# A graph kernel whose opening is put into another order: loads, node search, edge gathers and window masks

## The chip, the cores and the metric

The kernel runs on one core of a Trainium2 chip. A core has five engines that run their own instruction streams in order: TensorE (PE, matrix products and transposes, its weight loads shown apart as PEld), VectorE (DVE), ScalarE (ACT), GpSimd (POOL) and SyncE (SP). SP, ACT and POOL also issue DMA transfers, which 16 DMA engines carry out. Engines wait for each other by semaphores. The metric is device microseconds of one execution; lower is better.

## The reference, cut to what matters

There are 6250 nodes with 256 features, 100000 edges with 96 features, and `dst`, the node of each edge, in ascending order. A graph layer takes, for each node, the sum, the maximum and the mean of its edges' features, joins them to the normalised node features, and runs two dense layers. A mixture of 16 experts (two per node) follows.

```python
out1 = segment_sum(edge_attr, col)            # col = dst, sorted
cnt  = segment_sum(ones, col)
out2 = where(cnt > 0, segment_max(edge_attr, col), 0)
out3 = out1 / maximum(cnt, 1)
h = concatenate([x, out1, out2, out3, u[batch]], axis=1)     # x: layernorm of the nodes
x1 = x0 + relu(h @ W1 + b1) @ W2 + b2 + x
# then layernorm, top-2 of 16 experts, each 256 -> 512 -> 256, residual, layernorm
```

## The kernel before, in words

The 50 blocks of 125 nodes are cut into 13 groups: group 0 has two blocks, every other has four. Groups run from the last nodes to the first. For each group the hidden layer is computed in eight chunks (`hidden`, L772 and L789), then the output (`output`, L800), then the residual (L805), normalisation, gating and the scatter of rows to the experts. A list of tasks with slots (12 slots for a group) is sorted and run in order, so each engine's stream is fixed when the program is built. From slot 9 of the first two groups on, tasks are interleaved with the edge stream (`steps`, L316 to L320 on DVE), which makes running sums and maxima over all other edges and writes them to DRAM.

The nodes of groups 0 and 1 have few edges, at most 20 for a node. They don't use the edge stream. For each of their six blocks the kernel finds where a node's edges end and fetches the 20 rows before that point as a "window": 125 nodes by 20 rows by 96 features, 960 KB. This is done in steps:

- `load_all_ids` loads `dst` to 100 partitions (on ACT's queue). `block_starts` takes every 250th id and spreads it to all partitions by a matmul (L452 to L457).
- `find_block` (L486, ACT) counts for each node how many such ids lie below it; `take_blocks` (L490 to L492, DVE) makes an index, and an indirect DMA on POOL fetches the 250 ids at that place (L495, tile `gb`).
- `find_edge` (L502, ACT) counts within these ids; `bounds` (L512, L513), a pair of matmuls (`bounds_2`, L520, L521) and `index_windows` (L550 to L559, DVE) make window addresses and masks `mk`.
- `take_window` (L564, POOL) fetches a window by indirect DMA.
- `cut_window` (L572, ACT, ten small activations for half a window) or `cut_window_2` (L575, DVE, one operation for half a window) writes the window with foreign rows set to zero to a second tile. `sum_window` (L595, PE) sums it, and `add_window` (L602, DVE) folds the rest. `max_window` (L606 and L586, DVE) masks the window in place and takes its maximum; so it may begin only when the cuts have read the window. `mask_window` (L612, DVE) and `mean_window` (L617, L618, ACT) end the block.

For group 0 both engines cut, each into its own tile, `cut_w` or `cut_x`. For group 1 ACT cuts both halves, all four blocks into the one tile `cut_x`.

`check_order` (L265 to L267), `limits` and `check_fit` (L273 to L282) test whether the ids fit what the kernel was built for. The result, `misfit`, is loaded by every engine, and each branches on it (L1396, L1397): over a long block of general code that the ids of this reference don't need. Instructions on either side of that branch keep their side, save where a part of a step ended up ahead of it. Before the change, everything of groups 0 and 1 from `find_edge` on is written after the branch, although for group 0 the instructions up to L556 lie ahead of it in the streams. After the branch come also `root_x`, `scale_x` and `norm_x` (the layernorm of the nodes, L696, L702 to L704, L710), `find_block` for the four blocks of group 2 (L486), and the transposes of the normalised nodes (`turn`, L763, with the copy L764 on ACT).

DMA issues of SP and ACT share eight semaphores in turn, those of POOL eight others; a new issue waits until the transfer that used its semaphore before has landed.

Of the kernel before, what the change touches and what calls it, by code (L numbers as in the profile page):

```python
# [9 lines left out]
F32 = mybir.dt.float32  # L10
# [9 lines left out]
P = 125  # L20
# [3 lines left out]
WE = 20  # L24
# [6 lines left out]
GS = 4  # L31
# [14 lines left out]
def kernel(  # L46
# [18 lines left out]
    nc = tc.nc  # L65
# [402 lines left out]
    def more_constants():  # L468
        nc.vector.tensor_scalar(nhalf, node_i, -0.5, None, op0=OP.add)
        nc.vector.memset(rp[:, NT:], float(E))  # L470
        nc.vector.tensor_scalar(sh, row_i[:P, :P], 1.0, part_i[:P], op0=OP.add, op1=OP.is_equal)
        nc.vector.tensor_scalar(wrap, row_i[:P, :P], float(P - 1), None, op0=OP.is_equal)
        nc.vector.tensor_scalar(wrap, wrap, ident[:P, 0:1], None, op0=OP.mult)
        nc.vector.tensor_scalar(before, row_i, part_i, None, op0=OP.is_gt)
        nc.vector.memset(cnt_f, 0.0)
        nc.vector.memset(M[:, 0, :], 0.0)
# [8 lines left out]
        junk = ix.tile([P, NBK], BF16, name="junk")  # L485
        nc.scalar.activation(junk, b1r, AF.Sign, scale=-1.0, bias=nhalf[:, t:t + 1], accum_out=acc1[:, t:t + 1])  # L486

    def take_blocks(a, z):
        cols = slice(a, z)
        nc.vector.tensor_scalar(blk_f[:, cols], acc1[:, cols], float(NBK), 0.5, op0=OP.add, op1=OP.mult)  # L490
        nc.vector.tensor_scalar(blk_f[:, cols], blk_f[:, cols], -1.0, 0.0, op0=OP.add, op1=OP.max)
        nc.vector.tensor_copy(blk_i[:, cols], blk_f[:, cols])  # L492
        for t in reversed(range(a, z)):
            gbs_[t] = ix.tile([P, KB], I32, name="gb", bufs=6)
            nc.gpsimd.indirect_dma_start(out=gbs_[t], out_offset=None, in_=dst_b,  # L495
                                         in_offset=IndirectOffsetOnAxis(ap=blk_i[:, t:t + 1], axis=0))
# [75 lines left out]
            nc.scalar.activation(to[:, k, :], G[g]["win"][i][:, k, :], AF.Copy, scale=G[g]["mk"][:, i, 0, k:k + 1])  # L572

    def cut_window_2(g, i, k0, k1, to):
        nc.vector.tensor_tensor(to[:, k0:k1, :], G[g]["win"][i][:, k0:k1, :],  # L575
                                G[g]["mk"][:, i, 0, k0:k1, None].to_broadcast([P, k1 - k0, EF]), op=OP.mult)

# [99 lines left out]
    def take_x(g):  # L677
        a, z = GRP[g]
        xt = xall[:, g % XB]
        nc.sync.dma_start(xt[:, :z - a, 0:D], x[a * P:z * P].rearrange("(i p) d -> p i d", p=P))  # L680
        G[g]["xt"] = xt
# [531 lines left out]
    def at_slot(T, fn, *a, cost=0.0):  # L1213
        tasks.append((T, len(tasks), fn, a, cost))
# [21 lines left out]
    for g, (a, z) in enumerate(GRP):  # L1236
        B, n = SLOTS * g, z - a
        if g:
            if g > 1:
                at_slot(max(0, B - 17), take_x, g)  # L1240
                after = 5 if g == GW else 0
                at_slot(B - 14 + after, stats_x, g, 0, cost=1.2)
                at_slot(B - 13 + after, stats_x, g, 1, cost=1.2)
            if g > 1:
                at_slot(B - 11 + after, root_x, g)
                at_slot(B - 10 + after, scale_x, g, cost=0.5)
            at_slot(B - 9 + (4 if g == GW else 0), norm_x, g)
            for i in range(n):
                if g >= GW:
                    late = 3 if g == GW else 0  # L1250
                    at_slot(B - 10 + late + i // 2, take_edges, region[g], g, i)
                    at_slot(B - 9 + late + i // 2, take_carry, region[g], g, i)
                else:
                    for h in range(2):
                        at_slot(2 * i + h, cut_window, g, i, h * WE // 2, (h + 1) * WE // 2, None)
                        at_slot(2 * i + 1 + h, sum_half, g, i, h)
                    at_slot(2 * i + 1, max_window, g, i, cost=4.7)
                    at_slot(2 * i + 2, add_window, g, i, cost=0.9)
                    at_slot(2 * i + 2, mask_window, g, i, cost=0.4)
# [12 lines left out]
        early = GS - n  # L1272
        at_slot(B + SLOTS + 1 - early, root_b, g)
        at_slot(B + SLOTS + 2 - early, scale_b, g, cost=0.3)
        late = 0 if g >= NG - 2 else 1
        for k in range(DC):
            at_slot(B + SLOTS + 1 + k, turn_b, g, k)
        at_slot(B + SLOTS + 3 + late, logits, g)
        at_slot(B + SLOTS + 4 + late, choose, g, cost=2.4)
        at_slot(B + SLOTS + 5 + late, rank, g, cost=1.3)  # L1280
        at_slot(B + SLOTS + 6 + 2 * late, rank_2, g)
        at_slot(B + SLOTS + 7 + 2 * late, place, g, cost=1.5)
        for i in range(n):
            at_slot(B + SLOTS + 8 + 2 * late + i // 2, send, g, i)
# [37 lines left out]

    def fill_rows():

        nc.vector.memset(fill[:, D + 1:D + 5], 4.0 * NE * N)
        for h in range(SB // 128):
            nc.gpsimd.dma_start(xg_d.rearrange("(e n) d -> n e d", n=N)[h * 128:(h + 1) * 128],
                                fill[:, None, :].to_broadcast([128, NE, DR]))
# [5 lines left out]
    at_slot(SLOTS * (GW - 1) - 3, open_rows)  # L1334

    def loads_1():
        take_x(0)
        nc.sync.dma_start(w1x, w1[0:KC * 128].rearrange("(k p) h -> p k h", p=128))
        for q in range(4):
            nc.sync.dma_start(w1r[q * KR:(q + 1) * KR],  # L1340
                              w1[KC * 128:KC * 128 + KR].rearrange("k (j m n) -> k m j n", m=4, n=128)[:, q])
        take_x(1)
        load_ids(0)

    def loads_2():
# [22 lines left out]
    def windows_of(t, n):  # L1368
# [3 lines left out]
    a1, z1 = GRP[1]  # L1372
    base.append(chp.tile([P, RR, 2 * EF], F32, name="ct").rearrange("p r f -> p (r f)")[:, 0:(NT - W0) * 2 * EF]
                .rearrange("p (t f) -> p t f", f=2 * EF))
    w1u = wk.tile([P, GS, D], F32, name="xn", bufs=1).rearrange("p i d -> p (i d)")[:GF, 0:HID]
    cut_x = windows_of(xall[:, XB - 2:].rearrange("p b i d -> p (b i d)"), 1)[0]
    cut_w = w2s[:P].rearrange("p k d -> p (k d)")[:, 0:WE * EF].rearrange("p (k f) -> p k f", f=EF)
    with tc.manual_schedule():
        load_all_ids()
        loads_1()  # L1380
        nc.gpsimd.memset(base[0], 0.0)
        loads_2()
        more_constants()
        limits()
        nc.scalar.copy(gap, eps_t[0:1])
        nc.vector.memset(fill, 0.0)
        block_starts()
        check_order()
        for t in reversed(range(a, z)):
            find_block(t)  # L1390
        take_blocks(a, z)
        for t in reversed(range(a1, z1)):
            find_block(t)
        check_fit()
        take_blocks(a1, z1)
        bad_v = nc.values_load(misfit[0:1, 0:1])  # L1396
    with tc.If(bad_v != 0):  # L1397

# [39 lines left out]
        for t in range(NT - W0):  # L1438
            nc.vector.tensor_scalar(base[0][:, t, :], base[0][:, t, :], nw[:, t:t + 1], None, op0=OP.mult)
    with tc.manual_schedule():  # L1440
        global_part()
        stats_x(0, 0)
        for t in reversed(range(a, z)):
            find_edge(t)
        bounds(0)
        bounds_2(0)
        index_windows(0)
        for i in range(z - a):
            take_window(0, i, windows_of(w0p.tile([P, WE * EF], F32, name="w0"), 1)[0])
        root_x(0)  # L1450
        counts(0)
        for t in reversed(range(a1, z1)):
            find_edge(t)
        scale_x(0)
        norm_x(0)
        bounds(1)
        bounds_2(1)
        index_windows(1)
        for h in range(2):
            for w in windows_of(w1p.tile([P, 2 * WE * EF], F32, name="w1"), 2):  # L1460
                take_window(1, len(G[1].get("win", [])), w)
        stats_x(1, 0)
        stats_x(1, 1)
        root_x(1)
        scale_x(1)
        loads_3()
        for t in reversed(range(*node_cols(GW))):
            find_block(t)
# [98 lines left out]
```

## Time and profile before

| | |
|---|---|
| median of three runs | 1291.13 us (1291.03 to 1294.33) |
| the profiled execution | 1299.43 us, of which the span shown in the profile is 1297.6 us |
| busy, PE / DVE / ACT / POOL | 1113.4 / 963.4 / 612.6 / 558.8 us |
| instructions | 16883 |

Times in the profile are microseconds from the start of the span. A timeline line gives the start, the duration, the engine and line of kernel.py, the operation, what it writes and reads, the number of instructions merged, and in brackets how long the engine sat idle before it and what ended that. "DVEq" or "issue" as what ended it means the engine's own instruction queue, not another engine. In the table of stretches the columns are the length, then the busy time (and instructions) of PE, PEld, DVE, ACT and POOL, then PE's granted clock, the mean busy share of the 16 DMA engines, and GB/s.

### The profile page before, as it was taken

How to read it: one execution, taken by the hardware profiler on the slowest of the kernel's cores; microseconds unless marked ns; L12 is line 12 of the kernel's file. 1: busy time of each engine (PE TensorE's matmuls, PEld its weight loads, DVE VectorE, ACT ScalarE, POOL GpSimd, SP SyncE). 2: the span in 40 equal slices, each digit the busy share in tenths (PEclk: the TensorE clock that was granted, in tenths of full speed). 3: DMA queues.
4: the chain of work that ended last, by engine and by line, in shares of the span. 5: the costliest groups of instructions: out<-in, count | busy, mean ns of one | idle time of the engine just before them, and what ended most of it. 6: DMA issues, size and time to landing. Idle time of an engine off the chain costs nothing.

```text
span 1297.6 us, 16883 instructions
## 1 busy us (share of the span) xinstructions
PE 1113.4 (86%) x4637; PEld 783.4 (60%) x4637; DVE 963.4 (74%) x2754; ACT 612.6 (47%) x1449; POOL 558.8 (43%) x721
## 2 busy tenths in 40 slices
PE   2484796998789989899989999998999998989992
PEld 1252363655455554646646566886888777778881
DVE  4569787988988979999989422444377777778885
ACT  3484253662437542343424422432466666656662
POOL 4121142663347645375263333030145554545664
PEclk9897898999889998999999999998999999999996
DMA  5948785797779998898997331231677777778972
GB/s 163 209 108 234 206 242 160 204 242 208 216 222 267 252 244 228 235 255 228 274 260 237 90 95 42 66 100 50 195 229 228 231 238 252 254 228 254 280 259 73
DMA packets 179475, 261.25 MB, mean 201 GB/s; under 512 B 35915, under 2 KB 145963, under 8 KB 173729
## 3 DMA queue, kind: packets, MB, share of 16 engines
q1 hardware_dynamic: 140241, 202.23, 54.4%
q0 software_dynamic: 39008, 57.35, 16.1%
q8 instruction: 40, 0.66, 0.2%
q14 instruction: 74, 0.61, 0.2%
q10 hardware_dynamic: 112, 0.41, 0.1%
HBM read 146.70 MB, written 122.01 MB: 207 GB/s over the span
## 4 chain that ended last, share of the span: by engine, by line
PE 35%; DVE 13%; ACT 3%; DMA 3%; issue 3%; POOL 1%; POOLq 0%; SPq 0%; ACTq 0%; DVEq 0%
PE acc L1190 14%; PE acc L1166 11%; PE acc L772 5%; PE acc L800 3%; DVE yb L1089 2%; ACT yb L1091 2%; DVE rw L320 1%; DVE rw L317 1%; DVE rw L319 1%; DVE rw L316 1%; DMA xt<-in_x_dram 1%; ACT hb L1172 1%; DMA cg<-carry_d,next_i 1%; DMA xg_d<-xt,pos_i 1%; POOL xg_d L899 1%
## 5 line engine op out<-in xcount | busy, mean ns | idle before, releaser
L772 PE MATMUL acc<-inT,w1x 128*128 128x500 f32 (+1 forms) x832 | 369.0, 592 | 8.9 <-DVE xt L805 8.9
L772 PEld LDWEIGHTS acc<-inT,w1x 128*128 128x128 f32 x832 | 159.0, 199 | 169.7 <-issue 151.9
L1166 PE MATMUL acc<-xT,wt 128*128 128x256 f32 x912 | 223.2, 388 | 29.3 <-ACT hb L1172 25.7
L899 POOL DMA_INDIRECT xg_d<-xt,pos_i x100 | 134.4, 1344 | 250.2 <-DVE xt L895 119.8
L1190 PE MATMUL acc<-wt,hb 128*128 128x256 f32 x912 | 207.1, 380 | 0.0
L1166 PEld LDWEIGHTS acc<-xT,wt 128*128 128x128 f32 x912 | 169.2, 191 | 62.3 <-ACT hb L1172 38.1
L1190 PEld LDWEIGHTS acc<-wt,hb 128*128 128x128 f32 x912 | 174.1, 191 | 23.9
L800 PE MATMUL acc<-w2s,hT 128*125 128x256 f32 x800 | 186.5, 388 | 0.0
L800 PEld LDWEIGHTS acc<-w2s,hT 128*125 128x125 f32 x800 | 150.5, 193 | 23.7 <-issue 1.9
L1102 POOL DMA_INDIRECT g<-y_d,from_i x86 | 91.8, 1067 | 120.8 <-DMA y_d<-yb 90.5
L1135 POOL DMA_INDIRECT out_dram<-g,to_i x86 | 89.1, 1036 | 102.7 <-ACT hb L1172 86.5
L1091 ACT ACTIVATE yb<-yb,w_b 128x256 f32<-128x256 f32 x114 | 51.7, 501 | 154.0 <-DVE yb L1089 147.8
L495 POOL DMA_INDIRECT gb<-in_dst_dram,blk_i x50 | 74.1, 1483 | 114.2 <-issue 59.4
L1172 ACT ACTIVATE hb<-acc,wt 128x256 f32<-128x256 f32 x200 | 87.7, 464 | 49.5 <-PE acc L1166 41.0
L1089 DVE TENSOR_TENSOR yb<-acc,xe 128x512 f32<-128x512 f32 x57 | 39.4, 691 | 88.3 <-PE acc L1190 57.4
L794 ACT ACTIVATE hT<-acc,c 128x500 f32<-128x500 f32 (+1 forms) x104 | 60.1, 660 | 71.4 <-PE acc L789 71.4
L319 DVE TENSOR_TENSOR rw<-rw,raw 125x768 f32<-125x768 f32 x88 | 83.8, 953 | 0.0
L320 DVE TENSOR_TENSOR rw<-rw,raw 125x768 f32<-125x768 f32 x88 | 83.7, 951 | 0.0
L316 DVE TENSOR_TENSOR rw<-rw,keep 125x768 f32<-125x768 f32 x81 | 76.8, 948 | 5.0 <-DMA rows_d<-rw 4.9
L317 DVE TENSOR_TENSOR rw<-rw,bar 125x768 f32<-125x768 f32 x81 | 77.0, 950 | 0.0
L730 POOL DMA_INDIRECT at<-rows_d,first_i x44 | 61.6, 1399 | 34.2 <-issue 21.5
L737 POOL DMA_INDIRECT cg<-carry_d,next_i x44 | 63.2, 1437 | 25.7 <-issue 11.3
(313 smaller groups left out, 1577.9 us busy)
## 6 DMA issues: line engine op xcount, KB each, us to landing
wt<-in_wpack_dram SPq DMA_DIRECT2D x44, 1026.0 KB
rows_d<-rw SPq DMA_DIRECT2D x46, 960.0 KB
rows_d<-rw SPq DMA_DIRECT2D x46, 540.0 KB
raw<-in_edge_dram SPq DMA_DIRECT2D x46, 480.0 KB
xb<-xg_d SPq DMA_DIRECT2D x57, 263.0 KB
y_d<-yb SPq DMA_DIRECT2D x57, 256.0 KB
raw<-in_edge_dram SPq DMA_DIRECT2D x46, 270.0 KB
xt<-in_x_dram SPq DMA_DIRECT2D x12, 500.0 KB
```

The costliest lines, as they stand in the source:

```text
L316: nc.vector.tensor_tensor(su, prev[0], keep[c][:, :, s + j, None].to_broadcast(bcast), op=OP.mult)
L317: nc.vector.tensor_tensor(mx, prev[1], bar[c][:, :, s + j, None].to_broadcast(bcast), op=OP.min)
L319: nc.vector.tensor_tensor(su, su, x_j, op=OP.add)
L320: nc.vector.tensor_tensor(mx, mx, x_j, op=OP.max)
L772: nc.tensor.matmul(G[g]["pH"][m % 4][:, :n * P], w1x[:, k, m * 128:(m + 1) * 128], inT[:, k, :n * P], start=(k == 0), stop=False)
L800: nc.tensor.matmul(pO, G[g]["hT"][m][:, i * P:(i + 1) * P], w2s[:, m, :], start=(m == 0), stop=(m == HC - 1))
L899: d = nc.gpsimd.indirect_dma_start(out=xg_d[:, :], out_offset=IndirectOffsetOnAxis(ap=G[g]["pos"][:, i, k:k + 1], axis=0), in_=G[g]["xt"][ ...
L1102: d = nc.gpsimd.indirect_dma_start(out=g[:, h, :].bitcast(I32), out_offset=None, in_=y_d[:, :], in_offset=IndirectOffsetOnAxis(ap=BL[b]["f ...
L1135: d = nc.gpsimd.indirect_dma_start(out=out[:, :], out_offset=IndirectOffsetOnAxis(ap=BL[b]["to"][:, h:h + 1], axis=0), in_=g[:, h, :], in_ ...
L1166: nc.tensor.matmul(pB[i][:, half, :], wt[:, k * FF + m * 128:k * FF + (m + 1) * 128], xT[:, k, :], start=(k == 0), stop=(k == DC - 1))
L1172: nc.scalar.activation(hb[:, m, :], pB[i][:, half, :], AF.Relu, bias=bias)
L1190: nc.tensor.matmul(pY[:, h, :], hb[:, m, h * 128:(h + 1) * 128], wt[:, W2O + m * D:W2O + (m + 1) * D], start=(m == order[0]), stop=(m == o ...
```

## The change

- Loads: `take_x(0)` is issued on SP ahead of the ids (which are on ACT's queue); on SP, the nodes of group 1 and the small rest of W1 (`w1r`) now come before the 2 MB of W1 (`w1x`).
- `block_starts` is moved ahead of `limits`; the clearing of `fill` is moved from the opening to `fill_rows`, a task of slot 4.
- `check_order` comes after all six `find_block`, and `check_fit` after group 0's windows are requested. `take_blocks` gets an option `apart` that is not used.
- `find_edge`, `bounds`, `bounds_2`, `index_windows`, `take_window` of both groups and the node statistics `stats_x` of both are moved ahead of the branch.
- After the branch: both `root_x`, then `counts`, `scale_x`, `norm_x`, and then `global_part` (the eight products L1358 and the sum L1359).
- In group 1, ACT cuts the first half of each window and DVE the second, both in the same slot.
- `w1u` lies in a free node tile and no longer in the tile of `norm_x`.

```diff
@@ loads_1
-        take_x(0)
-        nc.sync.dma_start(w1x, ...)
+        take_x(1)
         for q in range(4):
             nc.sync.dma_start(w1r[q * KR:(q + 1) * KR], ...)
-        take_x(1)
+        nc.sync.dma_start(w1x, ...)
         load_ids(0)
@@ tasks of group 1
-                    for h in range(2):
-                        at_slot(2 * i + h, cut_window, g, i, h * WE // 2, (h + 1) * WE // 2, None)
+                    for h, fn in enumerate((cut_window, cut_window_2)):
+                        at_slot(2 * i, fn, g, i, h * WE // 2, (h + 1) * WE // 2, None)
@@ fill_rows
+        nc.vector.memset(fill, 0.0)
@@ the opening
     with tc.manual_schedule():
+        take_x(0)
         load_all_ids()
         loads_1()
...
+        nc.scalar.copy(gap, eps_t[0:1])
+        block_starts()
         limits()
-        nc.scalar.copy(gap, eps_t[0:1])
-        nc.vector.memset(fill, 0.0)
-        block_starts()
-        check_order()
         for t in reversed(range(a, z)):
             find_block(t)
         take_blocks(a, z)
         for t in reversed(range(a1, z1)):
             find_block(t)
+        check_order()
+        take_blocks(a1, z1)
+        stats_x(0, 0)
+        for t in reversed(range(a, z)):
+            find_edge(t)
+        bounds(0)
+        bounds_2(0)
+        index_windows(0)
+        for i in range(z - a):
+            take_window(0, i, ...)
         check_fit()
-        take_blocks(a1, z1)
+        stats_x(1, 0)
+        for t in reversed(range(a1, z1)):
+            find_edge(t)
+        stats_x(1, 1)
+        bounds(1)
+        bounds_2(1)
+        index_windows(1)
+        for h in range(2):
+            for w in windows_of(...):
+                take_window(1, len(G[1].get("win", [])), w)
         bad_v = nc.values_load(misfit[0:1, 0:1])
     with tc.If(bad_v != 0):
...
     with tc.manual_schedule():
-        global_part()
-        (stats, find_edge, bounds, windows of group 0)
         root_x(0)
+        root_x(1)
         counts(0)
-        (find_edge of group 1)
         scale_x(0)
         norm_x(0)
-        (bounds, windows, stats, root of group 1)
         scale_x(1)
+        global_part()
         loads_3()
```

In the resulting streams, DVE has the whole of L512 to L559 for both groups, `check_fit` and the six `stats_x` pairs ahead of its branch. PE has L1358 between the product of `check_fit` and the `bounds_2` of group 1. POOL has its six `gb` gathers and then its six windows without a branch in between, as before in that order. After the branch ACT has `norm_x(0)`, four L486, the copies L764 and the cuts, in that order as before.

More of the change, by code (lines that the diff above doesn't have):

```diff
@@ L486, in find_block, with take_blocks @@
         nc.scalar.activation(junk, b1r, AF.Sign, scale=-1.0, bias=nhalf[:, t:t + 1], accum_out=acc1[:, t:t + 1])
-    def take_blocks(a, z):
+    def take_blocks(a, z, apart=False):
         cols = slice(a, z)
@@ L492, in take_blocks, with gather_blocks @@
         nc.vector.tensor_copy(blk_i[:, cols], blk_f[:, cols])
+        if not apart:
+            gather_blocks(a, z)
+    def gather_blocks(a, z):
         for t in reversed(range(a, z)):
@@ L574, in cut_window_2 @@
     def cut_window_2(g, i, k0, k1, to):
+        to = cuts[0] if to is None else to
         nc.vector.tensor_tensor(to[:, k0:k1, :], G[g]["win"][i][:, k0:k1, :],
@@ L1336, in loads_1 @@
     def loads_1():
-        take_x(0)
-        nc.sync.dma_start(w1x, w1[0:KC * 128].rearrange("(k p) h -> p k h", p=128))
+        take_x(1)
         for q in range(4):
@@ L1341, in loads_1 @@
                               w1[KC * 128:KC * 128 + KR].rearrange("k (j m n) -> k m j n", m=4, n=128)[:, q])
-        take_x(1)
+        nc.sync.dma_start(w1x, w1[0:KC * 128].rearrange("(k p) h -> p k h", p=128))
         load_ids(0)
@@ L1374 @@
                 .rearrange("p (t f) -> p t f", f=2 * EF))
-    w1u = wk.tile([P, GS, D], F32, name="xn", bufs=1).rearrange("p i d -> p (i d)")[:GF, 0:HID]
+    w1u = xall[:, 2].rearrange("p i d -> p (i d)")[:GF, 0:HID]
     cut_x = windows_of(xall[:, XB - 2:].rearrange("p b i d -> p (b i d)"), 1)[0]
@@ L1393 @@
             find_block(t)
-        check_fit()
-        take_blocks(a1, z1)
+        check_order()
[7 more added lines that the diff above has]
+        for i in range(z - a):
+            take_window(0, i, windows_of(w0p.tile([P, WE * EF], F32, name="w0"), 1)[0])
+        check_fit()
+        stats_x(1, 0)
[6 more added lines that the diff above has]
+        for h in range(2):
+            for w in windows_of(w1p.tile([P, 2 * WE * EF], F32, name="w1"), 2):
+                take_window(1, len(G[1].get("win", [])), w)
         bad_v = nc.values_load(misfit[0:1, 0:1])
@@ L1440 @@
     with tc.manual_schedule():
-        global_part()
[L1442 to L1449, printed above, removed]
         root_x(0)
+        root_x(1)
         counts(0)
-        for t in reversed(range(a1, z1)):
-            find_edge(t)
         scale_x(0)
         norm_x(0)
[L1456 to L1464, printed above, removed]
         scale_x(1)
+        global_part()
         loads_3()
```

## The prediction

> **What bounds the kernel now.** I read the page's busy shares first: PE 86%, DVE 74%, so neither is full over the whole span. The change touches only the first 110 us, so I read the timeline there, then the stretches after it. The opening, in the timeline of the kernel before:
>
> ```profile
> 7.44 0.17 DVE L452 CAST dsf<-w 100x4 f32<-100x4 int32 x1 [1.12 <-DMA w<-in_dst_dram]
> ...
> 12.99 1.27 POOL L495 DMA_INDIRECT gb<-in_dst_dram,blk_i  x1 [7.83 <-DVE blk_i L492]
> ...
> 19.50 0.17 DVE L1359 TENSOR_TENSOR c<-ps,b1c 128x8 f32<-128x8 f32 x1 [3.29 <-PE ps L1358]
> ...
> 20.44 1.21 POOL L495 DMA_INDIRECT gb<-in_dst_dram,blk_i  x1 [4.62 <-DVE blk_i L492]
> ...
> 26.51 1.21 POOL L564 DMA_INDIRECT w<-in_edge_dram,win_i  x1 [0.31 <-issue]
> ...
> 28.15 0.18 DVE L558 TENSOR_SCALAR mk<-mk 125x40 f32<-125x40 f32 x1 [4.16 <-DVEq L1397]
> ...
> 30.55 0.17 DVE L529 TENSOR_SCALAR ne_n<-cnt 125x2 f32<-125x2 f32 x1 [1.68 <-issue]
> ...
> 31.46 1.09 ACT L710 ACTIVATE xn<-xt,nba,rsa 125x256 f32<-125x256 f32 x2 [1.88 <-issue]
> ...
> 36.37 0.30 ACT L696 ACTIVATE rsa<-mva,eps_t 125x4 f32<-125x4 f32 x1 [3.82 <-DVE mva L691]
> ...
> 41.19 2.76 ACT L572 ACTIVATE w2s<-w,mk 125x96 f32<-125x96 f32 x10 [0.26 <-DMA w<-in_edge_dram,win_i]
> ...
> 45.84 1.16 DVE L575 TENSOR_TENSOR xt<-w,mk 125x960 f32<-125x960 f32 x1 [3.50 <-DMA w<-in_edge_dram,win_i]
> 46.92 2.15 DVE L606 TENSOR_TENSOR w<-w,mk 125x1920 f32<-125x1920 f32 x1
> ```
>
> The reader is to see two paths that meet. One is the windows: requested at 26.51, first cut at 41.19, and DVE held until 45.84 by the second. The other is ACT, which at 41.19 had waited 0.26 us only: it had just come through `norm_x`, four searches and the transposes. Where the windows come earlier, ACT is late next. Group 1, by the same timeline:
>
> ```profile
> 68.50 2.16 DVE L606 TENSOR_TENSOR w<-w,mk 125x1920 f32<-125x1920 f32 x1 [8.53 <-ACT xt L572]
> ...
> 79.71 2.16 DVE L606 TENSOR_TENSOR w<-w,mk 125x1920 f32<-125x1920 f32 x1 [4.56 <-ACT xt L572]
> ...
> 98.55 2.16 DVE L606 TENSOR_TENSOR w<-w,mk 125x1920 f32<-125x1920 f32 x1 [4.75 <-ACT xt L572]
> ...
> 106.67 0.17 DVE L246 TENSOR_TENSOR keep<-di 125x48 f32<-125x48 int32 x1
> ```
>
> DVE sits idle for 17.8 us because ACT cuts both halves (2.76 us each). At 106.67 the edge stream begins. Stretches of the time that follows:
>
> ```profile
> 106.00:150.00 44.00, 21.99 (x56) 9.87 (x54) 41.42 (x87) 15.08 (x40) 9.89 (x8) 0.72 0.75 200
> 150.00:200.00 50.00, 46.65 (x175) 28.83 (x176) 40.12 (x165) 20.42 (x49) 18.41 (x18) 0.94 0.81 217
> ```
>
> DVE is busy 41.42 of 44 us, and PE waits for it; so an earlier 106.67 moves what follows.
>
> **Ids.** Let T be the moment DVE reads the ids, 7.44 before. The change takes the 2 MB of w1x from beside them and puts x of group 1 there, 500 KB. T lies between 5.4 (ids free of the 2 MB; DVE itself is free at 3.8) and 7.6 (nothing won, little lost). I take 6.9, near the measured row, since the ids had x of group 0 beside them in both.
>
> The Trainium skill ("DMA: Bandwidth & Descriptors", section on why a DMA increments its semaphore by 16) says that a transfer is spread over the largest number of engines up to 16 that divides its partitions, on SP and ACT the lowest-numbered: x with 125 partitions has five, which the ids on 99 share. By it T would stay 7.44 and the sum be 0.5 us smaller.
>
> **Windows of group 0.** The first gather leaves POOL at T+5.55, as before (12.99-7.44). Then DVE does `check_order`, three of 1.20 us, to T+8.8 (ACT's six searches at 0.755 us each end at T+7.7, so they hide beside it), and the second `take_blocks`, 0.6 us. The third gather leaves at T+9.75 instead of T+13.0, as `check_fit` and the wait for L1358 (3.29 us) are out of the way. Gathers go every 1.51 us, so the sixth is out at T+15.5 and the first window leaves at 22.7 instead of 26.51. From request to first cut took 14.7 us, to the second 17.8: landings at about 37.4 and 41 to 42, some 4 us earlier. `limits`, 2.3 us of DVE, hides beside the search; the 0.28 us of the fill is gone here and returns below.
>
> **The branch.** It now stands behind more. Gather two lands about 3.9 us after its issue (2.6 to 4.9 in the rows before), at 19.2; ACT and `bounds` give addresses 2.8 us later, 22.0, in time for POOL; masks end at 23.1. Then come `check_fit`, 3.56 us (12.58 to 16.14), and four statistics, 2.2 us: 28.9; `bounds`, 0.4. PE is in `global_part`, 3.57 us from 26.4 to 30.0, so `bounds_2` ends and DVE reads it at 31.0, 0.6 us lost to that order. Addresses and masks take 1.4 us: DVE is at its branch at 32.3 instead of 24.0, 8.3 us later. Group 1's first window leaves at 31.7 instead of 33.69, but is first needed at 60.
>
> After the branch DVE waited 4.16 us and after two further steps 1.68 us with nothing to wait for. I carry both over. Both bounds: nothing, as POOL issued across its branch after 0.31 us; and 9.37 us each, what a small gather took at 526.56 in the chain of waits, with the DMA engines busier than here. I take the rows themselves. From DVE's resume the old stream took 3.2 us to the factors of `norm_x`, less 0.5 us for the three instructions now ahead of the branch; so ACT starts `norm_x` at 39.4 instead of 31.46. From there it has 1.09 for `norm_x`, 2.9 for four searches, 1.5 for copy, transposes and copy: cut at 44.9 instead of 41.19. Before, it had 3.8 us of slack there (36.37); that cover is gone. The cut takes 2.76, so DVE's first maximum starts at 47.65 instead of 46.92: **0.7 us lost**, and the windows' 4 us not used. Two blocks of 6.0 us follow as before; group 0 ends at 59.7 instead of 58.98.
>
> The skill ("Runtime: NRT & Kernel Launch", section on instruction fetch) says that a taken branch out of the prefetched pages must fetch its target by DMA before it goes on. That speaks against this change, since six windows then load those engines; it has no figure for such a fetch.
>
> **Group 1.** Count from the end of group 0 (58.98 before, when L246 came 47.7 later). ACT's first cut ends at 6.85, as before 65.8, after copies and `keep_x`. DVE's own half, 1.16 us, lies in the idle time before. So the first maximum starts at 6.95 rather than 9.5. A block of DVE is 4.94 maximum, 0.65, 0.42, and now 1.16 for the next block's half: 7.1 us. Block one ends at 13.35 (its sum on PE is there at 12.2), the cut of block two at 14.45, b2 0.68 at 15.1. ACT has its half of block two at 11.7, so no wait. Maximum to 20.05; PE, with eight hidden products between sums and a wait for ACT's hT, has the sum at 20.3: 21.35. Cut, search index 0.6 and both clears 0.34: 23.4. ACT's half of block three came at 20.95. Maximum and fold to 29.4, cut to 30.55, the gate's work 1.95: 32.5 (ACT's half at 26.5). Maximum to 37.45. Now PE is late: its second-layer products (3.6 us) stand before the last sum, which comes at 38.8: fold to 39.9, b2 1.22, and 1.0 to L246 (as 105.7 to 106.67): 42.1 instead of 47.7. **5.6 us won.** Of the 11 us that ACT sheds and 17.8 us that DVE idled, 4.9 us are paid back as DVE's own cuts and clear, and the last sum takes part.
>
> **Sum.** -5.6 + 0.7 = -4.9 us. On the profiled execution, 1299.43 (span 1297.6 and 1.83 around it), that is 1294.5; on the median, 8.3 lower, 1286.2. The rest (w1x landing later, needed at 61; SP's branch, next needed at 48) costs nothing: at 61 the hidden products are 30 us behind any landing I can bound by the old 15.7 plus 6 for x.
>
> **Rivals.** *Slower: the branch stalls grow.* Every us that DVE resumes later comes out one for one, as ACT has no slack left. With 4.9 in hand, beyond 4.9 it is a loss, beyond 8.8 a measurable one. Both stalls at 9.37 instead of 4.16 and 1.68 are 12.9 us: 1299.1. For it: two to three windows are in flight then, where before the DMA share was about 0.35. Against: only a few fetches, and other queues got through while windows ran. *No change: the gain is given back.* One stall of 9.37 (5.2 more), or the time after 150, where DVE has 40.12 of 50 us and PE 46.65, so that a shift could end in another wait. It gives 1289 to 1292. Against it: the streams there are the same and all wait for each other, so they shift together. *More: no stall.* T at 5.4 and no fetch waits take 7.3 us from DVE's resume: ACT cuts at 37.6 to 40.4, the second window lands at 39.0 (requested at 21.2 + 17.8), and the first maximum starts at 40.4, 6.5 us earlier than before: 1279.0 at the far end, half of it 1282.6.
>
> **How the numbers follow.** Forecast 0.47 (its own range 1284 to 1289), no change 0.23, slower 0.17, more 0.13. About 0.3% (3.9 us) is what a measurement of this kernel can tell from none: 1287.3 and 1295.0. Of the forecast 0.42 lies below 1287.3, with the last case 0.55 faster; 0.05 and 0.23 make 0.28 the same; slower 0.17, of which I put two thirds above 1295. The range 1281.5 to 1295 leaves about 0.05 below and 0.13 above.
>
> **What would show it.** The third gather near 16.7 and the first window near 22.7; DVE's wait at its branch between 32 and 37; ACT's first cut near 45 with no wait for a window; DVE's waits for L572 in group 1 gone but one of about 5 us; L246 at 101 to 102. Wrong if ACT's cut waits for the windows still, if DVE resumes later than 41, or if L246 comes early and the end does not.

## The result, and the profile after

The changed kernel takes 1295.61 us (median of 20 runs, 1291.16 to 1301.12); the kernel before, run beside it, 1289.56 us (20 runs, 1285.34 to 1294.42). The ratio is 1.0046, 95% interval 1.0033 to 1.0059: about 6 us slower. The forecast was 1286.2 us, 4.9 us faster. In a later comparison, with other runs, the ratio was 1.0040 (1.0018 to 1.0062).

The timeline of the changed kernel, with the lines that answer those shown of the kernel before (start, duration, engine, line; in brackets the idle time ahead and what ended it):

```profile
6.78 0.17 DVE L452 CAST dsf<-w 100x4 f32<-100x4 int32 x1 [2.99 <-DMA w<-in_dst_dram]
...
16.89 1.21 POOL L499 DMA_INDIRECT gb<-in_dst_dram,blk_i  x1 [0.30 <-DVE bsa L695]
...
22.61 0.50 ACT L506 ACTIVATE junk<-gb,nhalf 125x250 bf16<-125x250 int32 x1 [0.45 <-DMA gb<-in_dst_dram,blk_i]
...
25.56 1.20 POOL L568 DMA_INDIRECT w<-in_edge_dram,win_i  x1 [2.92 <-DVE mk L560]
...
44.50 0.22 DVE L532 SCALAR_TENSOR_TENSOR cnt<-cnt,nf,cnt_f 125x2 f32<-125x2 f32 x1 [9.35 <-DVEq L1420]
...
51.62 0.23 DVE L537 TENSOR_SCALAR nw<-ne_n,nf 125x2 f32<-125x2 f32 x1 [6.42 <-issue]
52.14 1.09 ACT L715 ACTIVATE xn<-xt,nba,rsa 125x256 f32<-125x256 f32 x2 [20.20 <-DVE nba L708]
...
57.39 2.76 ACT L576 ACTIVATE w2s<-w,mk 125x96 f32<-125x96 f32 x10
60.19 2.16 DVE L611 TENSOR_TENSOR w<-w,mk 125x1920 f32<-125x1920 f32 x1 [5.45 <-ACT w2s L576]
...
79.12 2.16 DVE L611 TENSOR_TENSOR w<-w,mk 125x1920 f32<-125x1920 f32 x1 [4.78 <-ACT xt L576]
...
103.40 2.44 POOL L1333 DMA_DIRECT2D xg_d<-fill  x2
112.31 0.17 DVE L246 TENSOR_TENSOR keep<-di 125x48 f32<-125x48 int32 x1
119.96 11.13 SPq L329 DMA_DIRECT2D rows_d<-rw  x2
152.52 0.96 DVE L316 TENSOR_TENSOR rw<-rw,keep 125x768 f32<-125x768 f32 x1 [5.50 <-DMA rows_d<-rw]
```

Three things are to be seen. The two waits behind DVE's branch are 9.35 and 6.42 us instead of 4.16 and 1.68. ACT, which needs DVE's factor `nba`, is idle for 20.20 us, and the first maximum starts 13.3 us later than before (60.19 against 46.92). Group 1 then makes good 7.6 us: only one wait for ACT's cut is left, and from the end of group 0 to L246 it takes 40.1 us (72.25 to 112.31) where it took 47.7. Last, the edge stream, which begins 5.6 us late (112.31 against 106.67), loses about 5 us more at one place: DVE waits 5.50 us for a row buffer at 152.52, where the first profile of before had 0.55.

What was in flight when the engines stood at the branch, first in the kernel before, then in the changed one. The last three columns are PE's granted clock, the DMA share and GB/s:

```profile
20.00:25.00 5.00, 1.00 (x4) 0.91 (x4) 1.88 (x12) 3.08 (x7) 3.65 (x4) 1.00 0.40 114
25.00:30.00 5.00, 0.00 (x0) 0.00 (x0) 0.65 (x4) 2.18 (x8) 3.62 (x3) 1.00 0.35 87
```

```profile
35.00:40.00 5.00, 0.00 (x0) 0.00 (x0) 0.15 (x1) 0.00 (x0) 4.08 (x4) 1.00 0.88 199
40.00:45.00 5.00, 0.00 (x0) 0.00 (x0) 0.46 (x3) 0.00 (x0) 0.36 (x1) 1.00 0.99 220
45.00:50.00 5.00, 0.00 (x0) 0.00 (x0) 0.17 (x1) 0.00 (x0) 0.00 (x0) 1.00 1.02 257
```

In these 15 us PE and ACT do nothing and DVE 0.78 us, while the DMA engines are full.

The profiled execution of the changed kernel took 1297.04 us, less than the first profile of before (1299.43), which lay 8 to 10 us above its kernel's medians. A second profile of the unchanged kernel (below) explains this, and is the reference of the table that follows: how far the same matmul, counted from the first, starts later (+) or earlier (-) than in that second profile. It is worked out from the starts of the matmuls in the traces; "masks alone" is that kernel's second profile.

```
matmul  2nd profile  1st profile  changed  masks   masks and   changed,
        of before    of before             alone   fill early  fill early
  150      93.92       -2.70       +5.31   -8.01     -7.93       +4.77
  300     165.76       -2.92       +7.53   -7.07     -9.76       +2.82
  600     252.50       -4.83       +7.98   -7.88     -8.96       +3.73
 3300     974.16       -5.15       +8.27  -10.31    -10.83       -2.51
 4200    1167.11      +10.65       +8.28  -10.30    -10.87       -2.51
 last    1261.45      +10.77       +8.28  -10.30    -10.88       -2.50
```

The two profiles of the unchanged kernel differ by 1.2 to 7.4 us between 250 and 970 us, so the ends are read from the timed runs and the table only for where a shift arises. The four kernels that are compared below with 1302.19 us ran on a chip where the kernel before itself spread from 1283 to 1311 us, and their ratios leave out its longest runs, so that they are soft and don't follow from the medians; the traces carry the reading there.

### The profile page after: what moved, and what is told of

Read it like the earlier page. It is cut to its first block, busy times and chain, and to the rows that moved or that the text cites. A ratio compares the mean times of both kernels' runs of the same rounds, so it can differ in the third digit from the quotient of the medians.

```text
span 1295.2 us, 16845 instructions
## 1 busy us (share of the span) xinstructions
PE 1112.5 (86%) x4637; PEld 784.2 (61%) x4637; DVE 968.9 (75%) x2758; ACT 601.8 (46%) x1409; POOL 562.0 (43%) x721
## 4 chain that ended last, share of the span: by engine, by line
PE 32%; DVE 10%; ACT 4%; DMA 4%; issue 3%; POOL 1%; SPq 1%; POOLq 0%; DVEq 0%; ACTq 0%
PE acc L1195 14%; PE acc L1171 10%; PE acc L777 4%; DVE yb L1094 2%; PE acc L805 2%; DMA rows_d<-rw 2%; ACT yb L1096 2%; DVE rw L317 1%; ACT hb L1177 1%; DVE rw L320 1%; DVE rw L316 1%; DVE rw L319 1%; DMA cg<-carry_d,next_i 1%; DMA xg_d<-xt,pos_i 1%; ACT rsc L1125 1%
## 5 line engine op out<-in xcount | busy, mean ns | idle before, releaser
L805 PE MATMUL acc<-w2s,hT 128*125 128x256 f32 x800 | 190.2, 393 | 0.0
L805 PEld LDWEIGHTS acc<-w2s,hT 128*125 128x125 f32 x800 | 153.1, 196 | 24.8 <-issue 1.9
```

What stands on the lines that cost most here:

```text
L805: nc.tensor.matmul(pO, G[g]["hT"][m][:, i * P:(i + 1) * P], w2s[:, m, :], start=(m == 0), stop=(m == HC - 1))
```

## The experiments

### The masks alone, and the order alone

The kernel before with only the masks split, and the changed kernel without the split:

```diff
-                    for h in range(2):
-                        at_slot(2 * i + h, cut_window, g, i, h * WE // 2, (h + 1) * WE // 2, None)
+                    for h, fn in enumerate((cut_window, cut_window_2)):
+                        at_slot(2 * i, fn, g, i, h * WE // 2, (h + 1) * WE // 2, None)
```

> The kernel before, with only the masks of the first groups split between both engines (loads, gathers, checks and branch as before). Both theories agree here, since it measures the one term on which they rest: the second group's stage took 42.1 us in the sum and 40.5 us in the changed kernel's trace (L246 at 112.31, end of the first group at 71.83), against 47.7 us before. Theory A (the changed kernel loses its time at the branch, and the mask split is a gain): 5.6 to 7.6 us faster than before, ratio 0.994 to 0.996; the edge stream begins at about 99 to 101 us instead of 106.67. Theory B (what follows the opening gives any such gain back, so that an earlier stream start is worth nothing at the end): within 2 us of before.

> The changed kernel with the masks cut as before, by ScalarE alone: loads, order of the gathers and checks, and the late branch stay. Theory A (branch stalls): the first group's first maximum stays near 60 us (before 46.92), the group 1 stage goes back to about 47.7 us, the stream begins at about 120 us, 13 us later than before, and the end follows: 10 to 14 us slower than before, 1300 to 1304. Theory B (the stream swallows shifts of the opening): 4 to 8 us slower, as the changed kernel.

Masks alone: 1298.06 us against 1302.19, ratio 1.0026 (0.9977 to 1.0074), which settles nothing. L246 came at 98.92, as expected. (The 40.5 us of the expectation are the 40.1 us above, counted from the start of the last instruction of group 0 at 71.83.) Order alone: 1313.14 us, ratio 1.0098 (1.0062 to 1.0134). Its timeline:

```profile
43.45 0.22 DVE L532 SCALAR_TENSOR_TENSOR cnt<-cnt,nf,cnt_f 125x2 f32<-125x2 f32 x1 [8.25 <-DVEq L1420]
51.43 0.23 DVE L537 TENSOR_SCALAR nw<-ne_n,nf 125x2 f32<-125x2 f32 x1 [7.29 <-issue]
...
60.00 2.16 DVE L611 TENSOR_TENSOR w<-w,mk 125x1920 f32<-125x1920 f32 x1 [5.45 <-ACT w2s L576]
...
119.68 0.18 DVE L246 TENSOR_TENSOR keep<-di 125x48 f32<-125x48 int32 x1
```

The waits behind the branch are there without the split, and the stream starts 13.0 us later than before. So the change is two changes: an order that loses 13 us before the first maximum, and a split that wins 7.6 us behind it.

### Without the branch

The changed kernel, and the kernel before, without the `tc.If` block:

```diff
-        bad_v = nc.values_load(misfit[0:1, 0:1])
-    with tc.If(bad_v != 0):
-        ...
```

> The changed kernel without its branch and without the general code behind it, which serves other node ids than these; leaves that part out. Theory A (what the changed kernel loses, it loses in the stalls of DVE, ACT and SP at and behind the branch: 9.35 and 6.42 us on DVE): DVE's first maximum comes at 44 to 46 us instead of 60.19, bound then by the windows and ACT's cut, the stream begins near 97 to 99 us, and the kernel is 7 to 10 us faster than before. Rival C (the stalls only show a wait that is there anyway, as the landing of the windows or ACT's chain behind norm_x): the first maximum stays beyond 55 us and the time within 3 us of the changed kernel's. Rival D (the collisions in the edge stream, where DVE waits 9.7 us for rows_d instead of 4.9, come from the new load order and not from the shift): they stay, and the gain is 5 us smaller than A has it.

> The kernel before without its branch and the general code behind it; leaves that part out. It prices the branch where it stood before: VectorE's stalls were 4.16 and 1.68 us, but the windows held its first maximum until 46.92 all the same. Theory A (the cover is the landing of the windows): the first maximum comes at 43 to 46 us, 1 to 4 us earlier, and the time is 0 to 4 us below before. Rival T (the branch costs its stalls in full even there): 6 us or more below before.

The changed kernel without it: 1292.32 us against 1302.19, ratio 0.9918 (0.9878 to 0.9958). L246 came at 98.77, and DVE met no wait for its own instruction queue behind `bounds`; it waited for the windows:

```profile
40.78 1.16 DVE L580 TENSOR_TENSOR w2s<-w,mk 125x960 f32<-125x960 f32 x1 [5.99 <-DMA w<-in_edge_dram,win_i]
...
44.18 1.16 DVE L580 TENSOR_TENSOR xt<-w,mk 125x960 f32<-125x960 f32 x1 [2.09 <-DMA w<-in_edge_dram,win_i]
...
45.60 2.15 DVE L611 TENSOR_TENSOR w<-w,mk 125x1920 f32<-125x1920 f32 x1
```

This speaks against rival C: the first maximum comes 14.6 us sooner without the branch (45.60 against 60.19). Not all of it need be waits, since without the branch instructions from behind it also move forward in DVE's stream (L537 at 31.23, ahead of the addresses of group 1); the lighter windows below separate the two. The run also shows what the new order had to give without any stall: 45.60 against 46.92, 1.3 us. Rival D was half right: DVE's wait for a row buffer stayed (5.05 us at 138.53), so it isn't the branch's work, though it isn't the loads' either, as the masks alone show it too.

The kernel before without its branch: 1287.59 us against 1288.95, ratio 0.9997 (0.9974 to 1.0019). Its first maximum came at 47.45. Where the branch stood, its 5.8 us of waits cost nothing that these runs can tell (the interval ends some 3 us below before), since the windows landed later anyway. Theory A had the first maximum 1 to 4 us earlier; that was wrong, it came no earlier at all.

What the DMA engines carried from 34 to 50 us, by queue (packets, MB, share of 16 engines), in the changed kernel and then in the one without the branch:

```profile
q0 software_dynamic: 1358, 3.53, 92.3%
q14 instruction: 8, 0.07, 1.7%
```

```profile
q0 software_dynamic: 1329, 3.48, 93.7%
q14 instruction: 1, 0.01, 0.2%
```

The branch adds seven packets of instructions among some 1350 of windows and gathers. This fits the rule of the Trainium skill ("Runtime: NRT & Kernel Launch", section "Instruction fetch mechanics") that a taken branch out of the prefetched pages waits for a DMA. The times of the packets fit too: in the changed kernel an instruction packet ends at 49.99, and DVE's second wait at 51.62. In all seven profiles of the changed kernel or its variants in which DVE's second wait lasted over 5 us, it ended 1.61 to 1.66 us behind the end of such a packet. That the waits are those packets is still inferred, since the trace doesn't name the engine for which a packet came; the runs show that the waits need the branch and, below, the load.

### Lighter windows at the branch

The changed kernel's order, with the first four windows cut to one row of 20 (the rest of their tiles is cleared early). This kernel leaves out most of what these windows read, so its time says nothing about the change; its waits do:

```diff
-        nc.gpsimd.indirect_dma_start(out=w.rearrange("p k f -> p (k f)"), ...
+        nc.gpsimd.indirect_dma_start(out=w[:, 0:rows].rearrange("p k f -> p (k f)"), ...
```

> The changed kernel in its own order, but the first four windows fetch 1 of their 20 rows (the rest is cleared early), so that little is in flight when the engines come to the branch; leaves out most of what the first four blocks read. Theory A (the stalls at and after the branch grow with the transfers in flight): VectorE's wait at the branch goes from 9.35 back to 3 to 5 us, the second from 6.42 to 1 to 3, ScalarE's branch from 7.6 to about 3. Rival C (they belong to the place of the branch in the program or to what it is fetched from, whatever is in flight): they stay at 8 to 10 and 5 to 7 us.

One run of 1284.97 us. DVE's timeline, and the stretches of the stall:

```profile
40.80 0.22 DVE L532 SCALAR_TENSOR_TENSOR cnt<-cnt,nf,cnt_f 125x2 f32<-125x2 f32 x1 [3.72 <-DVEq L1424]
...
42.71 0.23 DVE L537 TENSOR_SCALAR nw<-ne_n,nf 125x2 f32<-125x2 f32 x1 [1.14 <-issue]
```

```profile
35.00:40.00 5.00, 0.67 (x4) 0.58 (x3) 1.21 (x7) 0.00 (x0) 2.42 (x2) 1.00 0.07 18
40.00:45.00 5.00, 0.91 (x2) 0.36 (x2) 2.92 (x14) 1.73 (x5) 2.42 (x2) 1.00 0.32 84
```

The branch stands at the same place in the program, behind the same work; what is in flight differs (and, with the clearing, the start). The waits fall from 9.35 and 6.42 us to 3.72 and 1.14, ACT's branch from 7.6 to 2.7. Theory A holds, and rival C falls. The first maximum came at 51.28, 8.9 us sooner than in the changed kernel. (With the early clearing DVE reads the ids at 11.89 and comes to its branch 1.9 us later, at 37.1.)

### The branch earlier

The changed kernel with the branch directly behind the first group's windows; the search, addresses and windows of group 1 and `global_part` stand behind it again, as before the change:

```diff
         take_blocks(a1, z1)
+        check_fit()
         stats_x(0, 0)
         ...
         for i in range(z - a):
             take_window(0, i, ...)
-        check_fit()
-        stats_x(1, 0)
-        ...
         bad_v = nc.values_load(misfit[0:1, 0:1])
```

> The changed kernel with the branch moved up: check_fit directly after the second take_blocks, then the first group's search and its two windows, then the branch; the second group's search, bounds, windows and statistics stand behind it as before the change. Loads, order of the gathers and the split masks stay. Theory A, with the stall growing with the transfers in flight at the branch: DVE reaches its branch at 26 to 29 us with two windows just asked for, the first stall is 4 to 6 us and the second 2 to 4, the first maximum comes at 47 to 51 us, and the kernel is 2 to 7 us faster than before. Rival E (the stall depends on which code is fetched, not on what is in flight, so it is about 9 and 6 us wherever the branch stands in this program): first maximum at 52 to 56 us, and the time 1 us faster to 3 us slower than before.

1302.69 us against 1302.19, ratio 0.9998 (0.9965 to 1.0030).

```profile
32.16 0.22 DVE L532 SCALAR_TENSOR_TENSOR cnt<-cnt,nf,cnt_f 125x2 f32<-125x2 f32 x1 [5.29 <-DVEq L1410]
...
38.47 0.23 DVE L537 TENSOR_SCALAR nw<-ne_n,nf 125x2 f32<-125x2 f32 x1 [5.62 <-issue]
...
51.20 2.16 DVE L611 TENSOR_TENSOR w<-w,mk 125x1920 f32<-125x1920 f32 x1 [4.33 <-ACT w2s L576]
```

The first wait was as theory A had it, the second longer (5.62 us against 2 to 4), and the time is where rival E had it (1 us faster to 3 slower), not theory A's 2 to 7 us faster. So this run alone doesn't decide between them; the lighter windows do. Two windows were on their way, with a DMA share of 0.62 and 0.53 from 30 to 40 us. The share over the wait itself goes roughly with its length: for the first wait 3.72 us (0.12, light windows), 4.16 (0.35, before), 5.29 (0.40, here) and 9.35 (0.93, changed); for the second 1.14 (0.35), 1.68 (0.31), 5.62 (0.63) and 6.42 us (1.01). Two windows in flight were enough to lengthen both, at a branch only 3 us later than before the change.

### The old loads

The changed kernel with the ids first, then x of group 0, w1x, w1r, x of group 1, as before the change.

```diff
-        take_x(0)
         load_all_ids()
         loads_1()     # x of group 0, w1x, w1r, x of group 1
```

> The changed kernel with the loads in their old order: x of group 0, the 2 MB of w1x, w1r, x of group 1, with the ids first. Theory A (order and masks set the time, the loads hardly do): ids read at 7.4 instead of 6.78, the first gathers issue in 1.2 instead of 2 us each and land 1 to 3 us sooner, the branch is reached within 2 us of the changed kernel's and the stalls stay above 12 us in sum: time within 3 us of the changed kernel. Rival H (w1x moved behind the gathers' addresses is what clogs the DMA engines at the branch): the two stalls fall to about 6 us in sum and the kernel is 8 us or more faster than the changed one.

1295.11 us, ratio 1.0046 (1.0026 to 1.0065), the changed kernel's own ratio. The ids were read at 7.59 us instead of 6.78, but the first window left at 25.57 against 25.56, and the waits were 8.84 and 6.79 us; rival H falls. The 0.8 us at the ids is within what executions differ by: the same changed kernel read them at 6.78 and, in its second profile, at 7.78. Over all profiles but that of the light windows it was 6.74 to 7.78 us with the new loads (seven, mean 7.30) and 7.44 to 8.26 with the old (ten, mean 7.75). So the new loads are worth some 0.4 us at the ids on average, and no gain behind them is seen.

### The kernel before, once more

> The kernel before, unchanged, for a second profile on another chip. In the expert stage (matmul 3300 to 4200) the first profile took 208.75 us, against 193.0 for the changed kernel. Theory F (this stretch differs from execution to execution of one and the same kernel): the second profile takes 5 us or more less, or lies otherwise off 208.75 by that much. Theory G (it belongs to the kernel): 206 to 211 us again. The ratio to the runs of before beside it is 1 within its interval in both.

1286.93 us, ratio 0.9982 (0.9963 to 1.0001). Matmuls 3300 to 4200 took 192.95 us, against 208.75 in the first profile and 192.96 in the changed kernel's: theory F. The 15.8 us by which the first profile is longer there belong to that execution; what brings such an execution about wasn't tried. The first maximum came alike (47.54), L246 2.7 us later (109.36).

### The fill of the expert rows

With the masks alone L246 came 7.75 us earlier than in the first profile of before, but by matmul 300 the lead was 3.2 us. The rows of before around the place, and of the masks alone in its second run:

```profile
94.33 2.45 POOL L1327 DMA_DIRECT2D xg_d<-fill  x2
...
113.98 7.66 SPq L329 DMA_DIRECT2D rows_d<-rw  x2
...
141.93 0.96 DVE L316 TENSOR_TENSOR rw<-rw,keep 125x768 f32<-125x768 f32 x1 [0.55 <-DMA rows_d<-rw]
```

```profile
89.68 2.44 POOL L1328 DMA_DIRECT2D xg_d<-fill  x2
...
98.99 0.18 DVE L246 TENSOR_TENSOR keep<-di 125x48 f32<-125x48 int32 x1
...
106.30 10.64 SPq L329 DMA_DIRECT2D rows_d<-rw  x2
...
137.87 0.96 DVE L316 TENSOR_TENSOR rw<-rw,keep 125x768 f32<-125x768 f32 x1 [4.18 <-DMA rows_d<-rw]
```

`fill_rows` sends 4.2 MB in two requests, in slot 4 of the plan. In the kernel before they left 12.3 us ahead of L246; with the split masks the stream comes sooner than POOL does, and they leave 9.3 us ahead (8.9 in the changed kernel). SP's first store of rows then takes 10.64 us to issue instead of 7.66, and the buffer comes free late. So the fill was moved:

```diff
-    at_slot(4, fill_rows)
+    at_slot(1, fill_rows)
```

> The masks-alone kernel (before with the masks of the first groups cut by both engines) with one more edit: the fill of the expert rows, 4.2 MB written by POOL's two requests, goes from slot 4 to slot 1 of the plan, so that it leaves near 65 to 70 us, where the DMA share is falling to 0.3, instead of 89.62. What it tests: the masks alone began the edge stream 7.75 us earlier than before (98.92 against 106.67) but were only 0.6 us ahead by matmul 600. Theory P (the fill still fills the DMA engines when the earlier stream writes its first rows: SP's first store took 12.41 us to issue against 7.66, and VectorE waited 5.35 us for a row buffer at 138.97 against 0.55): with the fill out of the way the first store issues in 2 to 6 us, the wait at that buffer is under 1 us, the lead at matmul 300 and at 600 is 8 to 13 us, and the time is 6 to 12 us below before. Theory Q (the stream is held by something else, as its own writes or PE): the lead at matmul 600 stays at 0 to 2 us and the time within 3 us of the masks-alone kernel.

> The masks-alone kernel once more, since its first comparison (1.0026, 0.9977 to 1.0074) settles nothing, on one chip with the two kernels that move the fill. Theory P (the mask split is worth its 7.75 us at the start of the edge stream, and the fill takes 3 to 5 of them back): 3 to 5 us below before, ratio 0.996 to 0.998; in the profile VectorE waits 5 us or so for the row buffer again. Theory Q (all of it is given back): within 1.5 us of before.

> The kernel before with only the fill moved from slot 4 to slot 1. Theory P: before the change the fill (issued at 94.33) was nearly through when the first rows were written (113.98, wait of 0.55 us for the row buffer), so moving it wins little by itself: 0 to 2.5 us faster. Rival R (the gain of the kernel with both edits is the fill's alone): 7 to 10 us faster.

> The changed kernel with the fill moved from slot 4 to slot 1. Theory P (besides the branch stalls the changed kernel loses 4.3 us in the edge stream where the first rows meet the fill, VectorE's wait 5.50 us at 152.52): the wait falls under 1 us, the stalls stay at 9 and 6 us, and the time is 3 to 5 us below the changed kernel's: 1 to 3 us above before. Rival S (this wait comes from something else in the new order): as the changed kernel, 5 to 7 us above before.

| kernel | median, us | before beside it | ratio and interval |
|---|---|---|---|
| masks, fill early | 1278.74 | 1288.82 | 0.9918 (0.9891 to 0.9945) |
| masks alone, again | 1282.61 | 1288.95 | 0.9960 (0.9941 to 0.9979) |
| fill early alone | 1288.18 | 1288.95 | 1.0006 (0.9988 to 1.0025) |
| changed, fill early | 1290.46 | 1288.95 | 1.0028 (1.0005 to 1.0051) |

The masks with the fill early:

```profile
71.42 2.44 POOL L1328 DMA_DIRECT2D xg_d<-fill  x2 [31.65 <-DVE fill L1326]
...
99.07 0.18 DVE L246 TENSOR_TENSOR keep<-di 125x48 f32<-125x48 int32 x1
...
106.38 7.72 SPq L329 DMA_DIRECT2D rows_d<-rw  x2
...
135.04 0.96 DVE L316 TENSOR_TENSOR rw<-rw,keep 125x768 f32<-125x768 f32 x1 [1.28 <-DMA rows_d<-rw]
```

The fill lands while the stream hasn't begun, the first store issues in 7.72 us, and the wait is 1.28. In the changed kernel with the fill early (84.14) the store took 7.68 and the wait was 1.03 us. The expected 2 to 6 us for the store and under 1 us for the wait were too low; with the fill gone the store, two requests of 960 KB, still takes as long as before the change. The fill alone wins nothing, as theory P said and against rival R: before, it was out of the way in time. The masks alone are a gain, 5 us on this chip, against theory Q.

How much of the wait reaches the end was still open, since the kernels ran on different chips. Four of them side by side on one:

> The changed kernel, beside the three others on one chip. Both theories: 5 to 7 us above before.

> The masks-alone kernel on the same chip. Both theories: 4 to 7 us below before.

> The masks-alone kernel with the fill in slot 1, on the same chip. Theory P (the wait that meets the fill reaches the end): 3 to 5 us below the masks-alone kernel. Theory U (most of it is made good later, where the stream waits for other stores all the same, as the 4.2 to 4.3 us at its second row buffer in every profile): 0 to 1.5 us below it.

> The changed kernel with the fill in slot 1, on the same chip. Theory P: 3 to 5 us below the changed kernel. Theory U: 0 to 1.5 us below it.

| kernel | median, us | ratio to before (1291.59 us) |
|---|---|---|
| changed | 1296.89 | 1.0040 (1.0018 to 1.0062) |
| changed, fill early | 1291.68 | 1.0008 (0.9982 to 1.0033) |
| masks alone | 1284.55 | 0.9944 (0.9922 to 0.9966) |
| masks, fill early | 1281.04 | 0.9915 (0.9889 to 0.9942) |

For the changed kernel the difference of the means is 4.8 us (with twice its standard error, 2.4 to 7.3, worked out from 12 runs each): theory P, theory U falls. For the masks it is 3.1 us (-0.2 to 6.5, six runs each), and that is not settled: in the two pairs of profiles the early fill is 2.7 and 2.1 us ahead at matmul 300, but 0.6 and 0.1 us at the last matmul, which is what theory U says. The masks split in the old order, with the fill early, are the best version found: 0.9918 and 0.9915 of before, some 10 us, without the new loads, the new order or the moved branch.

## Why the prediction was wrong

- **Ids and the third gather:** 6.78 us (6.9 forecast) and 16.89 (16.7), the first in part by luck: the changed kernel's second profile has 7.78 for the ids. The rule drawn from the skill ("DMA: Bandwidth & Descriptors", section on why a DMA increments its semaphore by 16) would have left them where they were; the means, 7.30 us with the new loads and 7.75 with the old, speak for some gain, but executions of one kernel differ by more, so the runs don't decide.
- **"Gather two lands ... at 19.2":** too early. ACT read the second gather at 22.61, the first at 21.57 after waiting 7.15 us. The first two requests took 1.93 and 2.02 us of POOL instead of 1.27 and 1.25, with old and new loads alike. The first window left at 25.56 instead of 22.7, 1 us sooner than before instead of 4, and DVE came to its branch at 35.1 instead of 32.3. That is 2.8 us.
- **"I carry both over ... I take the rows themselves":** the step that failed most. The rows 4.16 and 1.68 us had been measured at a DMA share of 0.35 and 0.31. The same change put all six windows ahead of the branch in the program: three had been requested when DVE came there, the others followed while it waited. The share over the waits was 0.93 and 1.01, and they lasted 9.35 and 6.42 us: 9.9 us more. The text named those windows and the bound of 9.37 us, and gave this rival a chance of 0.17; its mechanism is what happened. The 2.8 and 9.9 us, less 0.2 us by which ACT was quicker from `norm_x` to its cut (5.25 us against 5.5), make up the 12.5 us by which the first maximum (60.19) came behind the forecast (47.65). That every us of a later resume comes out one for one was right: ACT had no slack left.
- **Group 1:** right in kind, the gain too small. The stage took 40.1 us, not 42.1, and one wait of 4.78 us for ACT was left, as forecast. PE was hardly late at the last sum (DVE waited 0.23 us for it).
- **"An earlier 106.67 moves what follows" and the streams "shift together":** failed for a shift that comes out of group 1. DVE, busy 41.42 of 44 us, was read as the bound of 106 to 150; the DMA share of 0.75 beside it was not asked about. The fill of 4.2 MB, tied to a slot of group 1 and to POOL's queue, didn't move with the stream, and the first stores met it. That cost the changed kernel 4.6 to 4.8 us by matmul 300, against the two profiles of before, and moving the fill gave 4.8 us (2.4 to 7.3) at the end. A shift that the fill shared, as with the order alone, went through: the fill left 13.5 us later, the stream started 13.0 us later, and matmul 300 came 13.6 us later.
- **The sum:** -4.9 us was +0.7 for group 0 and -5.6 for group 1. Against the first profile of before it was +13.3, -7.6 and +4.8 in the stream, +10.4 by matmul 300; against the second +2.95 at the start of the stream and +7.5 by matmul 300. The timed runs say +6.0. The first profile of before lost 15.8 us in the expert stage that its second doesn't have, and ended 10.8 us later; the 8.3 us taken off for the median were near that.

## What to carry to other kernels

A wait that is copied from the profile holds only for the load under which it was measured: when a change moves transfers ahead of a branch, price the branch under those transfers. When one stage is shortened, ask which large transfer is tied to the old place in the plan and will now meet the stage behind it; moving that transfer into an idle stretch was worth 4.8 us in the changed kernel (2.4 to 7.3), perhaps 3 with the masks alone, and nothing measurable without the shortening. And split a bundle of edits before believing in it: here one edit won 5 to 7 us and the rest lost 11 to 13.

## What the runs showed of the hardware

- The wait of DVE at the branch over the general code grew from 3.72 us at a DMA share of 0.12 to 9.35 us at 0.93, and a second wait four instructions behind it from 1.14 us at 0.35 to 6.42 at 1.01. In six profiles with the changed kernel's order and load the two lasted 8.25 to 9.35 us and 6.19 to 7.29 us. In the changed kernel ACT's wait at the branch lasted 7.6 us and SP's 6.7.
- The unchanged kernel's group 1 took 47.7 us in one profile and 49.8 in another. Between 85 and 90 us PE's granted clock was 1.00 in the first and 0.66 in the second, and ACT's copy there waited 2.29 us for PE instead of 0.92. With the masks split, L246 came at 98.9 to 100.0 us in five profiles; with ACT cutting alone in the old order, at 106.7 to 110.9 in four. So against three of these four the split brings the stream 9 to 12 us ahead, not the 7.7 us of the pair first compared. Whether the lower clock is the reason wasn't tried.
- One and the same kernel took 193 or 209 us for matmuls 3300 to 4200. In the long execution PE and its weight loads waited 42.6 us for ACT's `hb` between 985 and 1190 us, in the changed kernel's short one 9.3 us; why is open.
